# Attention over a graph on one core: 16 instead of 14 of 52 pairs weighted on GpSimd, and another order on TensorE

## The chip, the core and the metric

The kernel runs on one core of a Trainium2 chip. A core has five engines that work beside each other, each through its own queue in order: TensorE (matrix products, its weight loads listed apart), VectorE, ScalarE, GpSimd, and SyncE, which here only starts transfers. Matrix products land in PSUM, everything else lives in SBUF. The metric is the device time of one execution in microseconds (us), the median of three runs.

## The reference

The input is 3327 nodes with 128 features and a dense 0/1 adjacency matrix. Layer 0 is a graph convolution with batch norm and takes little of the time. Layer 1 is an attention whose score gets the adjacency added twice, because it is passed both as spatial and as edge encoding:

```python
x = x + _L0_gnn_ref(h, adj, ...)               # graph convolution, batch norm, relu
h = jnp.maximum(_layernorm(x, axis=-1), 0.0)
q = (h @ Wq.T).reshape(d, n, heads)            # d = 128, n = 3327, heads = 8
k = (h @ Wk.T).reshape(d, n, heads)
v = (h @ Wv.T).reshape(d, n, heads)
a = jnp.einsum('dnh,dmh->dnm', q, k) * d ** (-0.5)
a = softmax(a + adj + adj, axis=2)
out = jnp.einsum('dnm,dmh->dnh', a, v).reshape(n, heads * d)
x = x + out @ Wo.T
```

So there are 128 independent attentions ("d"), each with 3327 queries, 3327 keys and a head size of only 8.

## The kernel before

The first 291 us hold layer 0, the second norm and the first projections. Then `attention()` runs one long unrolled list of steps. It takes the 128 attentions in 32 groups of 4 (`G`), the queries in 7 blocks (six of 512 columns and one of 255), and the keys in 26 chunks of 128. A *pair* is one chunk for two of the four attentions, so a block has 52 pairs; `half` 0 is attentions 0 and 1, `half` 1 is attentions 2 and 3. A block is cut into 13 steps (`SU`) of four pairs: 32 x 7 x 13 = 2912 steps in all. A loop entry is (i, y, s): group, block, step.

One pair goes like this. `product` (L718) makes two score matmuls for a chunk, one for each attention; each uses 32 rows of the array (`rs`, L724: rows 64 half + 32 x), where q and k hold high and low parts of 8 features. They go to one of three score slots in PSUM (`psc`, tile `s`). Then there are two ways to exp(2 x (score + adj)):

- *plain*: VectorE adds the adjacency and a bound to the scores (`add`, L815, tile `d`, L818 in the profile). One ScalarE `Exp` over all plain pairs of a step follows a step later (`late`, L854, L856 in the profile).
- *rest* (`weighted`, L825): ScalarE takes `Exp` of the scores alone (tile `f`, L828), and GpSimd multiplies it by exp(2 adj) (L831), which was stored in DRAM as `wd` and is fetched as `wt`.

`pairs(s)` (L682) says which pairs of a step are which: three plain and one rest, in the last step two and two. Chunks 0 to 18 are plain, chunks from `WC` = 19 on are of the second kind: 14 of 52 pairs. Chunk numbers are arranged so that successive pairs change the half.

The sum over keys is `weigh` (L603): a matmul of a pair's weights with v, one call for each of its two attentions, whose nine output rows lie at 32b, b = 0 to 3, of the block's PSUM bank `av`. In the trace each call is two matmuls. It runs three steps (`LAG`) after the scores: `second(part)` (L776) handles pairs 0 and 1 of the waiting step, then pairs 2 and 3. After a block's last step `finish` (L609) runs in stages through `step()`: VectorE copies `av` to `avs`, TensorE makes four transposes (L619), VectorE divides (L626 to L629), a transfer stores the result.

The order is written out by hand: engines execute in the order in which the loop issues. Within a step (L838 to L852) TensorE gets: scores of the rest pair, scores of plain 0, `second(0)` (four calls), scores of plain 1, scores of plain 2 (or of a second rest pair), guests from `beside`, `second(1)` (four calls). `step()` stands after `second(0)`.

`beside` (L756) lets in guests at fixed steps: projections of the next group (L196, with VectorE's copies and GpSimd's casts behind them) and the output product of the last group (L257, L265). `fetch(x + PRE)` issues transfers two steps ahead on SyncE's queue: `at` (two adjacency chunks) and `wt` (one weight chunk). `weigh_early` and `more_weights` make `wd`: the first `EARLY` = 3 blocks before the loop, the others during group 0. `loads` brings in q, k and v of the next group, with GpSimd casts for k (L180).

Of the kernel before, what the change touches and what calls it, by code (L numbers as in the profile page):

```python
# [22 lines left out]
NC = 26  # L23
T = N * D
NP = NC * P
NB = 512
# [2 lines left out]
HALF = 0.5 / math.sqrt(D)  # L29
SAFE = 30.0  # L30
SU = NC // 2
WC = 19
CH = 4 * NP // D
NG = D // G
EARLY = 3

# [6 lines left out]
def tile_two_layer_gnn(  # L45
# [22 lines left out]
    blocks = [(n0, min(NB, N - n0)) for n0 in range(0, N, NB)]  # L68
# [58 lines left out]
    sets = [tile_set(x) for x in range(2)]  # L127
# [158 lines left out]
    with tc.tile_pool(name="l0", bufs=1) as l0, tc.tile_pool(  # L286
# [125 lines left out]
        for c in range(NC):  # L412
            a = ap.tile([P, 7 * NB], F32, name="a")
# [15 lines left out]
            i = c - 2 * NQ - 5  # L429
            if 0 <= i < NQ - 2 and 4 * i + 4 <= c:  # L430
                spread(i)
        weights = []
        for y, (n0, w) in enumerate(blocks[:EARLY]):
            a = ap.tile([P, 7 * NB], F32, name="a")
            a7 = a.rearrange("p (c n) -> p c n", c=7)
            nc.sync.dma_start(a7[:, :, :w], adjr[:, WC:, n0 : n0 + w])
            weights.append((a7, n0, w))

# [50 lines left out]
        for i, (n0, w) in enumerate(blocks):  # L489
            s = slice(n0, n0 + w)  # L490
# [78 lines left out]
        q, k, v = sets[0]  # L569
# [11 lines left out]
        for x, c in enumerate(range(0, NC, 4)):  # L581
            n = min(4, NC - c)
# [20 lines left out]
    def weigh(tiles, av, w, e, b, c, first, last):  # L603
        nc.tensor.matmul(  # L604
            av[32 * b : 32 * b + H + 1, :w], tiles[2][:, b, c, :], e,
            start=first, stop=last,
        )
# [44 lines left out]
    def attention():  # L652


        with tc.tile_pool(name="adj", bufs=4) as ap, tc.tile_pool(
# [17 lines left out]
            if True:  # L673
                steps = [
                    (i, y, s)
                    for i in range(NG) for y in range(len(blocks)) for s in range(SU)
                ]
# [4 lines left out]
                def pairs(s):  # L682


                    last = s == SU - 1
                    plain = [(j // 2, j % 2) for j in range(3 * s, 3 * s + 3 - last)]
                    rest = [(WC + s // 2, 1 - s % 2)]
                    return plain, rest + ([(NC - 1, 0)] if last else [])


                wanted, have = [], {}
                for x, (i, y, s) in enumerate(steps):
                    n0, w = blocks[y]
                    for c, _ in pairs(s)[0]:
                        if (0, i, y, c // 2) not in have:
                            have[0, i, y, c // 2] = None
                            wanted.append((x, 0, i, y, c // 2))
                    c = pairs(s)[1][0][0]
                    if (1, i, y, c) not in have:
                        have[1, i, y, c] = None  # L700
                        wanted.append((x, 1, i, y, c))

                def fetch(x):
                    while wanted and wanted[0][0] <= x:
# [13 lines left out]
                def product(i, y, c, half):  # L718
                    q, k, _ = sets[i % 2]
                    n0, w = blocks[y]  # L720
                    we = w + w % 2
                    p = psc.tile([P, 2, NB], F32, name="s")
                    for x in range(2):
                        rs = slice(64 * half + 32 * x, 64 * half + 32 * x + 32)  # L724
                        nc.tensor.matmul(  # L725
                            p[:, x, :we], k[rs, c, :], q[rs, n0 : n0 + we],
                            start=True, stop=True,
                        )
                    return p
# [26 lines left out]
                def beside(i, y, s):  # L756


                    for j in [1, 2] if i == 0 else [i + 2] if i + 2 < NG else []:
                        if (y, s) != (0 if i else 3 * (j - 1), 3):  # L760
                            continue
                        hj = wk.tile([P, CH], F32, name="hj")
                        nc.sync.dma_start(hj, hd[:, j * CH : (j + 1) * CH])
                        extra.extend(projections(wk, hj, j, False, ov, low_half[:CH, 1:2]))
                    if s in (8, 11) and extra:
                        drive(extra[0])
                    if s in (9, 12) and extra:
                        drive(extra.pop(0))
                    if s in (7, 10) and extra:
                        drive(extra[0], avs2[(i * len(blocks) + y + 1) % 2])  # L770
                    if (y, s) == (2, 12) and i:
                        extra.extend(outputs(wk, i - 1))

                extra = []

                def second(part):  # L776

                    (i, y, s), es = waiting[0]
                    n0, w = blocks[y]
                    av = avs2[(i * len(blocks) + y) % 2]  # L780
                    ps = sum(pairs(s), [])
                    for j in (0, 1) if part == 0 else (2, 3):
                        c, half = ps[j]
                        for x in range(2):
                            weigh(
                                sets[i % 2], av, w, es[j][:, x, :w], 2 * half + x, c,
                                s == 0 and part == 0, s == SU - 1 and part == 1,
                            )
                    if part:
                        waiting.pop(0)  # L790
                        if s == SU - 1:
                            ending.append(finish(rp, av, at(i), n0, w))

                def step():
                    for g in ending[:1]:
                        if next(g, g) is g:
                            ending.pop(0)

                for x, (i, y, s) in enumerate(steps):
                    n0, w = blocks[y]  # L800
                    fetch(x + PRE)
                    k = x - i * SU * len(blocks) - FROM[i]
                    if k == 0 and i + 1 < NG:
                        pending = loads(sets[(i + 1) % 2], at(i + 1))
                        total = len(pending)

                    while pending and (total - len(pending)) * (SU * len(blocks) - FROM[i] - 4) <= k * total:
                        pending.pop(0)()
                    more_weights(i, y, s)
                    due = len(waiting) == LAG  # L810
                    plain, rest = pairs(s)
                    d = ep.tile([P, 3, 2, NB], F32, name="d")
                    es = [d[:, j] for j in range(len(plain))]

                    def add(j, p):  # L815
                        c = plain[j][0]

                        nc.vector.scalar_tensor_tensor(  # L818
                            d[:, j, :, :w],
                            have[0, i, y, c // 2][:, c % 2, :w]  # L820
                            .unsqueeze(1).to_broadcast([P, 2, w]),
                            SAFE / 2, p[:, :, :w], ALU.min, ALU.add,
                        )

                    def weighted(c, half):  # L825
                        f = fp.tile([P, 2, NB], F32, name="f")
                        p = product(i, y, c, half)
                        nc.scalar.activation(  # L828
                            f[:, :, :w], p[:, :, :w], AF.Exp, scale=2.0
                        )  # L830
                        nc.gpsimd.tensor_tensor(  # L831
                            f[:, :, :w], f[:, :, :w],
                            have[1, i, y, c][:, :w].unsqueeze(1).to_broadcast([P, 2, w]),
                            ALU.mult,
                        )
                        es.append(f)

                    weighted(*rest[0])  # L838
                    if late is not None:
                        late()  # L840
                    add(0, product(i, y, *plain[0]))
                    if due:
                        second(0)
                    step()
                    add(1, product(i, y, *plain[1]))
                    if len(rest) > 1:
                        weighted(*rest[1])
                    else:
                        add(2, product(i, y, *plain[2]))
                    beside(i, y, s)  # L850
                    if due:
                        second(1)  # L852

                    def late(d=d, w=w, n=len(plain)):  # L854
                        flat = d[:, :n].rearrange("p j x n -> p (j x) n")[:, :, :w]
                        nc.scalar.activation(flat, flat, AF.Exp, scale=2.0)  # L856

                    waiting.append(((i, y, s), es))
                late()
                while waiting:  # L860
                    second(0)
                    step()
                    second(1)
                while ending:
                    step()
                for p, b in zip(outputs(wk, NG - 1), (0, 1, 0)):
# [197 lines left out]
```

## Time and profile before

| what | us |
|---|---|
| median of three runs | 10516.94 (10514.26 to 10520.51) |
| the profiled execution's own time | 10527.91 |
| its span, first to last instruction | 10526.1 |
| `d` adds on VectorE, L818, 512 wide, x7296 | 8417.5 busy, 1213 ns each |
| `d` exponentials on ScalarE, L856, three pairs, 512 wide, x2304 | 6398.3 busy, 2777 ns each |
| the same, two pairs, x192 | 372.5 busy, 1940 ns each |
| `f` exponentials on ScalarE, L828, 512 wide, x2688 | 2753.2 busy, 1032 ns each |
| `f` products on GpSimd, L831, 512 wide, x2688 | 6412.7 busy, 2394 ns each |
| score matmuls on TensorE, L725, 512 wide, x19968 | 499 ns each |
| av matmuls from `d`, L604, 512 wide, x29184 | 600 ns each |
| mean granted TensorE clock | 0.986 |

The profile cuts the span in 40 slices; each digit is a busy share in tenths (9 is 90% or more):

```profile
PE   7889999999999999999999999999999999999999
DVE  5789999999999999999999999999999999999998
ACT  4889999999999999999999999999999999999998
POOL 0667777777777777777777777777777777777776
```

PE is TensorE, DVE VectorE, ACT ScalarE, POOL GpSimd; PEld stands for TensorE's weight loads, which are listed as a row of their own. The picture is the same from the second slice to the last, so one block stands for all. Busy times on one engine may overlap slightly: the next instruction begins before the one ahead of it is recorded as ended, and so the distance between starts tells more than a mean duration. In a line of a timeline there are, from the left, the start, the duration of what is merged in the line, the engine, the line of the kernel, the operation, the tile written and the tiles read, the shapes, the count, and in brackets how long the engine was idle before and what ended that.

### The profile page before, as it was taken

To read this page: it belongs to the slowest core of one execution; us is meant where nothing else is said; L and a number is where in the kernel's file an instruction comes from. 1 tells how busy PE (TensorE), PEld (TensorE's weight loads), DVE (VectorE), ACT (ScalarE), POOL (GpSimd) and SP (SyncE) were. 2 spreads that over 40 slices of the span, in tenths; PEclk is the share of its full clock that TensorE was granted. 3 is DMA by queue.
4 is the path that set the end of the run, shared out by engine and by line. 5 is a ranking of instruction groups with operands and counts; after the bars stand their busy time and mean duration, and the time that the engine had idled before them with its cause. 6 is when DMAs were issued, how large, how long until landed. Compare 5 with 4: busy or idle time off the path is not lost. (4 is left out here: it accounts for less than half of the span.)

```text
span 10526.1 us, 186778 instructions
## 1 busy us (share of the span) xinstructions
PE 9922.7 (94%) x72399; PEld 2813.8 (27%) x72399; DVE 9714.9 (92%) x9949; ACT 9948.5 (95%) x6200; POOL 7497.1 (71%) x3868
## 2 busy tenths in 40 slices
PE   7889999999999999999999999999999999999999
PEld 3222222222222222222222222222222222222222
DVE  5789999999999999999999999999999999999998
ACT  4889999999999999999999999999999999999998
POOL 0667777777777777777777777777777777777776
PEclk8899999999999999999999999999999999999999
DMA  7655555555555555555555555555555555555554
GB/s 241 192 168 163 157 168 165 163 162 160 162 166 165 164 162 157 161 170 163 160 162 157 165 170 165 160 158 163 164 169 163 162 163 158 165 165 167 156 152 128
DMA packets 1115761, 1731.67 MB, mean 165 GB/s; under 512 B 198350, under 2 KB 441932, under 8 KB 1107180
## 3 DMA queue, kind: packets, MB, share of 16 engines
q1 hardware_dynamic: 1110478, 1713.99, 56.3%
q8 instruction: 568, 9.31, 0.4%
q10 hardware_dynamic: 4350, 5.64, 0.2%
q14 instruction: 333, 2.73, 0.1%
q0 software_dynamic: 32, 0.00, 0.0%
HBM read 1618.76 MB, written 100.53 MB: 163 GB/s over the span
## 5 line engine op out<-in xcount | busy, mean ns | idle before, releaser
L818 DVE SCALAR_TENSOR_TENSOR d<-at,s 128x1024 f32<-128x1024 f32 x8512 | 9204.3, 1138 | 642.7 <-PE s L725 406.2
L831 POOL TENSOR_TENSOR f<-f,wt 128x1024 f32<-128x1024 f32 (+1 forms) x3136 | 6983.8, 2235 | 2619.1 <-ACT f L828 2572.0
L856 ACT ACTIVATE d<-d 128x3072 f32<-128x3072 f32 (+1 forms) x2912 | 7372.9, 2532 | 73.4 <-DVE d L818 70.5
L604 PE MATMUL av<-d,v 128*9 128x512 f32 x34048 | 5528.5, 569 | 0.1
L725 PE MATMUL s<-q,k 32*128 32x512 f32 x23296 | 4280.7, 482 | 505.7 <-DVE d L818 218.0
L725 PEld LDWEIGHTS s<-q,k 32*128 32x128 f32 x23296 | 1773.9, 182 | 5829.2 <-DVE d L818 3312.2
L828 ACT ACTIVATE f<-s 128x1024 f32<-128x1024 f32 (+1 forms) x3136 | 3014.8, 970 | 313.8 <-PE s L725 252.3
L604 PE MATMUL av<-f,v 128*9 128x512 f32 x12544 | 2864.0, 571 | 0.0
L604 PEld LDWEIGHTS av<-d,v 128*9 128x9 f32 x34048 | 630.7, 88 | 1381.6 <-issue 1265.4
L604 PEld LDWEIGHTS av<-f,v 128*9 128x9 f32 x12544 | 310.6, 88 | 52.9 <-issue 41.0
L180 POOL CAST k<-ks 128x256 fp32r<-128x256 f32 x434 | 284.2, 655 | 0.0
L416 PE MATMUL acc<-a,A 128*128 128x512 f32 (+1 forms) x364 | 151.3, 568 | 24.0 <-ACT A L350 23.3
L619 PEld LDWEIGHTS av<-ident,avs 128*128 128x128 f32 (+1 forms) x864 | 121.1, 208 | 179.9 <-issue 178.8
L226 POOL TENSOR_TENSOR o<-pf,o 104x512 fp32r<-104x512 f32 x124 | 160.4, 1293 | 9.9
L619 PE MATMUL av<-ident,avs 128*128 128x128 f32 (+1 forms) x864 | 163.8, 311 | 0.6 <-DVE avs L612 0.6
L225 POOL CAST o<-pf 104x512 fp32r<-104x512 f32 x124 | 75.8, 611 | 115.3 <-DVE pf L224 59.8
L612 DVE COPY avs<-av 128x512 f32<-128x512 f32 (+1 forms) x224 | 144.2, 644 | 2.8 <-PE av L604 2.8
L423 DVE TENSOR_REDUCE amax<-a 128x1 f32<-128x3327 f32 x26 | 93.7, 3610 | 37.7 <-DMA a<-in_adj 37.7
L416 PEld LDWEIGHTS acc<-a,A 128*128 128x128 f32 x364 | 68.8, 192 | 108.8 <-issue 84.4
L420 ACT ACTIVATE junk<-a 128x3327 bf16<-128x3327 f32 x26 | 77.4, 2977 | 6.6 <-DMA a<-in_adj 6.5
L389 POOL TENSOR_TENSOR sq<-wk 128x512 f32<-128x512 f32 x2 | 2.1, 1040 | 102.3 <-PE aside L390 102.3
L629 DVE TENSOR_TENSOR oq<-av,ri 128x128 f32<-128x128 f32 (+1 forms) x224 | 64.1, 286 | 7.7
(120 smaller groups left out, 952.0 us busy)
## 6 DMA issues: line engine op xcount, KB each, us to landing
at<-in_adjT SPq DMA_DIRECT2D x1728, 512.0 KB
wt<-wd SPq DMA_DIRECT2D x1344, 256.0 KB
at<-in_adjT SPq DMA_DIRECT2D x288, 255.0 KB
ks<-kT SPq DMA_DIRECT2D x496, 104.0 KB
q<-qT SPq DMA_DIRECT2D x496, 104.0 KB
at<-in_adjT SPq DMA_DIRECT2D x192, 256.0 KB
a<-in_adj SPq DMA_DIRECT2D x26, 1663.5 KB
wt<-wd SPq DMA_DIRECT2D x224, 127.5 KB
```

The source lines that it names most:

```text
L180: nc.gpsimd.tensor_copy(k[:, c : c + n, half * 64 : half * 64 + 64], ks.bitcast(F32).rearrange("g (p c) -> g c p", c=NC)[:, c : c + n, :],)
L226: nc.gpsimd.tensor_tensor(o[:CH, 1], f[:CH], o[:CH, 0].bitcast(F32), ALU.subtract)
L416: nc.tensor.matmul(acc[i][:, :w], A[:, c, :], a[:, n0 : n0 + w], start=(c == 0), stop=(c == NC - 1),)
L423: nc.vector.tensor_reduce(amax[:, c : c + 1], a[:, :N], AX.X, ALU.max, apply_absolute_value=True)
L604: nc.tensor.matmul(av[32 * b : 32 * b + H + 1, :w], tiles[2][:, b, c, :], e, start=first, stop=last,)
L612: nc.vector.tensor_copy(avs[:, :w], av[:, :w])
L619: nc.tensor.transpose(pt[:R, j, :], avs[:, j : j + (R - 1) * J + 1 : J], ident)
L725: nc.tensor.matmul(p[:, x, :we], k[rs, c, :], q[rs, n0 : n0 + we], start=True, stop=True,)
L818: nc.vector.scalar_tensor_tensor(d[:, j, :, :w], have[0, i, y, c // 2][:, c % 2, :w] .unsqueeze(1).to_broadcast([P, 2, w]), SAFE / 2, p[:, ...
L828: nc.scalar.activation(f[:, :, :w], p[:, :, :w], AF.Exp, scale=2.0)
L831: nc.gpsimd.tensor_tensor(f[:, :, :w], f[:, :, :w], have[1, i, y, c][:, :w].unsqueeze(1).to_broadcast([P, 2, w]), ALU.mult,)
L856: nc.scalar.activation(flat, flat, AF.Exp, scale=2.0)
```

## The change

`pairs(s)` now reads a table `kinds`. Steps 4, 8 and 12 (`DOUBLE`) have two plain and two rest pairs, the other ten three and one; so 36 pairs are plain and 16 rest, and `WC` becomes 18. `beside` moves VectorE's part of the guests into steps 8 and 12 (their later part to step 9 and to step 0 of the next block), and the matmul of the second guest from step 10 to 11.

On TensorE the order in a step becomes: `second(0)` (two calls), scores of plain 0, `second(1)`, `step()`, `second(2)`, scores of plain 1, `second(3)`, scores of plain 2 (or of the second rest pair), scores of the next step's first rest pair (`coming`), guests. `second` now handles one pair a call.

The early weights cover two blocks instead of three, 1024 columns in three pieces of 342 with 8 chunks each, in place of three pieces of 512 with 7 chunks; block 2 is left to the loop.

```diff
-WC = 19
+WC = 18
-EARLY = 3
+DOUBLE = (4, 8, 12)
+EARLY = 2
...
-        for y, (n0, w) in enumerate(blocks[:EARLY]):
+        w = -(-EARLY * NB // 3)
+        for n0 in range(0, EARLY * NB, w):
             a = ap.tile([P, 7 * NB], F32, name="a")
-            a7 = a.rearrange("p (c n) -> p c n", c=7)
+            a7 = a.rearrange("p (c n) -> p c n", c=8)
...
                 def pairs(s):
-                    last = s == SU - 1
-                    plain = [(j // 2, j % 2) for j in range(3 * s, 3 * s + 3 - last)]
-                    rest = [(WC + s // 2, 1 - s % 2)]
-                    return plain, rest + ([(NC - 1, 0)] if last else [])
+                    return kinds[s]
+
+                kinds = []
+                for s in range(SU):
+                    j, k = (sum(len(x[i]) for x in kinds) for i in range(2))
+                    n = 2 if s in DOUBLE else 1
+                    kinds.append((
+                        [(x // 2, x % 2) for x in range(j, j + 4 - n)],
+                        [(WC + x // 2, 1 - x % 2) for x in range(k, k + n)],
+                    ))
...
-                    c = pairs(s)[1][0][0]
-                    if (1, i, y, c) not in have:
-                        have[1, i, y, c] = None
-                        wanted.append((x, 1, i, y, c))
+                    for c, _ in pairs(s)[1]:
+                        if (1, i, y, c) not in have:
+                            have[1, i, y, c] = None
+                            wanted.append((x, 1, i, y, c))
...
-                    if s in (8, 11) and extra:
+                    if s in (8, 12) and extra:
                         drive(extra[0])
-                    if s in (9, 12) and extra:
+                    if s == 9 and extra or s == 0 and (y or i) and begun:
                         drive(extra.pop(0))
-                    if s in (7, 10) and extra:
+                        begun.pop()
+                    if s in (7, 11) and extra:
+                        begun.append(1)
                         drive(extra[0], avs2[(i * len(blocks) + y + 1) % 2])
...
-                def second(part):
+                def second(j):
+                    if not due:
+                        return
                     (i, y, s), es = waiting[0]
...
-                    for j in (0, 1) if part == 0 else (2, 3):
-                        c, half = ps[j]
-                        for x in range(2):
-                            weigh(
-                                sets[i % 2], av, w, es[j][:, x, :w], 2 * half + x, c,
-                                s == 0 and part == 0, s == SU - 1 and part == 1,
-                            )
-                    if part:
+                    c, half = ps[j]
+                    for x in range(2):
+                        weigh(
+                            sets[i % 2], av, w, es[j][:, x, :w], 2 * half + x, c,
+                            s == 0 and j < 2, s == SU - 1 and j >= 2,
+                        )
+                    if j == 3:
                         waiting.pop(0)
...
+                def first(x):
+                    i, y, s = steps[x]
+                    return product(i, y, *pairs(s)[1][0])
+
+                coming = first(0)
                 for x, (i, y, s) in enumerate(steps):
...
-                    def weighted(c, half):
+                    def weighted(c, p):
                         f = fp.tile([P, 2, NB], F32, name="f")
-                        p = product(i, y, c, half)
...
-                    weighted(*rest[0])
+                    weighted(rest[0][0], coming)
                     if late is not None:
                         late()
+                    second(0)
                     add(0, product(i, y, *plain[0]))
-                    if due:
-                        second(0)
+                    second(1)
                     step()
+                    second(2)
                     add(1, product(i, y, *plain[1]))
+                    second(3)
                     if len(rest) > 1:
-                        weighted(*rest[1])
+                        weighted(rest[1][0], product(i, y, *rest[1]))
                     else:
                         add(2, product(i, y, *plain[2]))
+                    if x + 1 < len(steps):
+                        coming = first(x + 1)
                     beside(i, y, s)
-                    if due:
-                        second(1)
```

More of the change, by code (lines that the diff above doesn't have):

```diff
@@ L772, in beside @@
                         extra.extend(outputs(wk, i - 1))
-                extra = []
-                def second(part):
+                extra, begun = [], []
+                def second(j):
+                    if not due:
+                        return
                     (i, y, s), es = waiting[0]
@@ L859, in attention @@
                 late()
+                due = True
                 while waiting:
-                    second(0)
+                    for j in range(4):
+                        second(j)
                     step()
-                    second(1)
                 while ending:
```

## The prediction

> **What bounds the kernel now.** I read the page's busy times and groups first, then the list of waits, then the timelines of ScalarE, of TensorE's weight loads and of its matmuls in single steps of the loop (a step is four pairs; a block has 13 steps, a group 7 blocks, there are 32 groups).
>
> ```profile
> PE 9922.7 (94%) x72399; PEld 2813.8 (27%) x72399; DVE 9714.9 (92%) x9949; ACT 9948.5 (95%) x6200; POOL 7497.1 (71%) x3868
> PEld s L725 <- DVE d L818: 3312.2, 4433, 6.4
> PEld s L725 <- ACT f L828: 1197.0, 1922, 11.8
> ```
>
> Three engines look full. But TensorE's loads for the scores `s` stand still 3312.2 us for VectorE and 1197.0 us for ScalarE, which free the score slots: those two set the pace, and TensorE's 94% is not work. ScalarE's timeline in full-width steps:
>
> ```profile
> 3101.64 1.08 ACT L828 ACTIVATE f<-s 128x1024 f32<-128x1024 f32 x1
> 3102.54 2.84 ACT L856 ACTIVATE d<-d 128x3072 f32<-128x3072 f32 x1
> 3105.20 1.08 ACT L828 ACTIVATE f<-s 128x1024 f32<-128x1024 f32 x1
> ```
>
> Start to start, `f` takes 0.90 and `d` 2.66 us: 3.56 a step. VectorE has three adds of about 1.16 (three in 3.48 us at 3100.09), 3.5 us, and stretches the steps that bring it a copy or a reciprocal. Successive `avs` copies, one a block, lie 46.96 and 48.33 us apart (3048.64, 3095.60, 3143.93), against 12 x 3.56 + 3.65 = 46.4 us of ScalarE.
>
> What TensorE needs by itself, from its weight loads, the first instruction of each phase:
>
> ```profile
> 3101.79 0.12 PEld L604 LDWEIGHTS av<-d,v 128*9 128x9 f32 x8 [0.24 <-issue]
> 3102.77 0.19 PEld L725 LDWEIGHTS s<-q,k 32*128 32x128 f32 x4 [0.86 <-DVE d L818]
> 3103.20 0.10 PEld L604 LDWEIGHTS av<-d,v 128*9 128x9 f32 x3 [0.25 <-issue]
> ...
> 3104.18 0.18 PEld L725 LDWEIGHTS s<-q,k 32*128 32x128 f32 x2 [0.86 <-DVE ri L627]
> 3105.45 0.18 PEld L725 LDWEIGHTS s<-q,k 32*128 32x128 f32 x2 [1.08 <-DVE d L818]
> 3105.88 0.12 PEld L604 LDWEIGHTS av<-d,v 128*9 128x9 f32 x8 [0.24 <-issue]
> 3106.85 0.19 PEld L725 LDWEIGHTS s<-q,k 32*128 32x128 f32 x4 [0.86 <-ACT f L828]
> ```
>
> An `av` phase (two pairs, four `weigh` calls, eight matmuls, since each call is two) takes 3101.79 to 3102.77 = 0.98 us. A score phase of four matmuls takes 0.43 (3102.77 to 3103.20). A score phase of which only two were left takes 0.43 as well (3105.45 to 3105.88). So the number of matmuls in a phase is not its price. The matmuls say why:
>
> ```profile
> 3103.21 0.60 PE L604 MATMUL av<-d,v 128*9 128x512 f32 x2
> 3103.22 0.60 PE L604 MATMUL av<-f,v 128*9 128x512 f32 x2
> 3103.64 0.60 PE L604 MATMUL av<-d,v 128*9 128x512 f32 x2
> 3103.65 0.60 PE L604 MATMUL av<-f,v 128*9 128x512 f32 x2
> ```
>
> Four start together, and 0.43 later the other four: the four calls lie in four column strips (32b, b = 0 to 3) and run side by side; only the two matmuls of one call follow each other. That a call alone is no cheaper is seen at a projection:
>
> ```profile
> 3013.99 0.26 PEld L196 LDWEIGHTS av<-wv,hj 128*104 128x104 f32 x2 [0.24 <-issue]
> 3015.02 0.10 PEld L604 LDWEIGHTS av<-d,v 128*9 128x9 f32 x3 [0.78 <-issue]
> ```
>
> One call, 1.03 us. In 255-wide blocks (at 10489.92, 10490.24 and 10490.79 in the same timeline) the phases are 0.32 and 0.55. From widths 512 and 256 a score phase is about 0.21 fixed plus 0.22 of streaming.
>
> Before, a step is two cycles of (score, av): 2 x 1.41 = 2.82 us, and a block 26 x 1.41 + 0.67 (four transposes, 3002.09 to 3002.76) + 1.3 of guests = 38.6 us against 47 to 48. TensorE has 9 us to spare in each block.
>
> **What the Trainium skill says.** "TensorE: Matmul & The Clock Gate", Part 3, The mechanism: matmuls on different row or column strips run concurrently, but all start and end in program order. The trace agrees with the first (starts 0.01 apart). By the second, four calls share the time only if nothing stands between them. "TensorEngine Tiling (Array Packing)", Key Properties: changing the tiling mode drains the array. The trace agrees: `s` (32*128) never overlaps `av` (128*9), and each change shows a bare load, 0.19 or 0.12. "Trainium Kernel Development and Optimization", Performance Expectations: matmul busy time is a bad measure of distance to the limit; here 94% busy holds 38.6 us of need in 48.
>
> **The change, part by part.**
>
> *Order on TensorE.* Before: av of two pairs twice a step. After: av j0 | s plain0 | av j1, j2 | s plain1 | av j3 | s last and s coming | ... So three cycles of phases a step, not two. j0 and j3 stand alone, two calls in two strips, each call's two matmuls still serial: 2 x 0.43 + 0.12 = 0.98, as a full phase. s plain0 and plain1 alone: 0.43 each, as measured. No run of before has a lone av pair: below it could be 0.43 if half-filled phases went at double speed, above 0.98; I take 0.98, for the projection above goes no faster alone. Full width: 39 cycles x 1.41 = 55.0 us a block. 255 wide: 39 x 0.87 = 33.9.
>
> *Halves.* From `kinds`: in 10 of 13 steps (all but 4, 8, 12) the last pair of a step and `coming` have the same half, so the same two row strips, and run one after the other. Unseen in before, where every score phase has both halves. Below 0 (if they overlap after all), above 0.40 (0.19 load and 0.22 streaming: the page's same section lets a load overlap only other row strips); I take 0.21, streaming alone, since in the first layer's row of matmuls loads of the same strips are hidden (one start each 0.43, load 0.19). 10 x 0.21 = 2.1 us; 255 wide 1.1. In the double steps j1 and j2 have the same half, so the same column strips: 0.86 more, at s = 7, 11 and 2, three steps later: 2.6 us; 255 wide 1.3. Bounds 0.8 to 1.0.
>
> *Transposes.* `step()` now stands between second(1) and second(2), so at s = 4 the four transposes part j1 from j2: 0.98 more (0.55 narrow), beside their own 0.67.
>
> Sum: 55.0 + 2.1 + 2.6 + 0.98 + 0.67 = 61.3 us full, 33.9 + 1.1 + 1.3 + 0.55 + 0.67 = 37.5 narrow. A group 6 x 61.3 + 37.5 = 405.3, 32 of them 12,970. Guests as before: 186 projections x 1.04 = 193, 31 outputs x (2 x 0.50 + 1.93) = 91 (3063.84 to 3064.34, 3110.78 to 3112.71). Outside the loop: 297 us before its steps run and 20 after the last av (the chain ends 10505.98 to 10526). 12,970 + 284 + 317 = 13,571 span, 1.8 more as the profiled run's time, and the median of the runs lies 11 below that: 13,560.
>
> *VectorE.* 36 adds, not 38: 2 x 1.16 = 2.3 us a block less, and copies moved into the steps with two adds (8 and 12). Worth nothing: 36 x 1.16 + 1.4 (`finish`) + 0.8 of guests = 44 us, beside 61 of TensorE.
>
> *ScalarE.* 10 x 3.56 + 3 x (0.90 + 1.83 + 0.91) = 46.5 us, hidden. *GpSimd.* 16 x 2.39 = 38.3 us and its casts, hidden.
>
> *Slots.* With three score slots each product waits for the third before it. By the phases above (step of 4.42): plain0 at 0.98, plain1 at 2.39, last at 3.80. Add 0 ends at about 2.7, add 1 at 4.1, add 2 at 5.5; plain0 of the next step comes at 5.4 and needs add 1: free. plain1 at 6.8 needs add 2: free. The next `coming`, behind which that step's j0 is queued, needs add 0: long done. In a step with a 0.68 copy add 2 ends near 5.7: still free. I count no stall; if this cover failed by 0.1 a step it would be 290 us.
>
> *Loads and start.* `at` fetches 9, not 10, a block, `wt` 8, not 7: the same columns in all, on the same SP queue in the same places. DMA is at half use. The early weights go as three DMAs of 8 x 342 for 7 x 512, and in group 0 block 2's are made in the loop, some 8 ScalarE calls of 1.15: at most 9 us, hidden by a lag of three steps. Early part: within 10 us either way; I take 0.
>
> **Rivals.**
> 1. *Partial overlap* (12,580): lone av pairs or same-half scores cost less than a phase. With 0 for the halves of the scores (6 x 2.1 x 32 + 1.1 x 32 = 440 less) and 0.10 less in each lone av phase (2 x 13 x 0.10 x 6 x 32, half of it narrow: 540 less). Against it: both prices come from starts in the trace.
> 2. *Faster*: TensorE stays hidden, and what VectorE gives up counts. It needs lone phases that cost what their matmuls weigh, half: 26 x (0.49 + 0.21) = 18.2 us less, 43.1 a block, under ScalarE's 46.5. A block then goes from 48.4 on average ((319.0 a group - 28.5 narrow) / 6) to 46.5: 1.9 x 192 = 365 us, so 10,150. It decides at 46.5 us of TensorE per block; with only the av half as dear it is 48.6, which is no change. For it: VectorE's stretched steps are real. Against: the 1.03 of a lone call and the 0.43 of a lone score pair.
> 3. *A further wait comes on top* (14,050 to 14,500): 0.40 for same-half scores (+400), or a stall of 0.1 to 0.2 a step. For it: only half a score phase lies between some frees and their use if ScalarE slips.
>
> **How the numbers follow.** Forecast 0.79, rival 1 0.09, rival 2 0.04, rival 3 0.08. The forecast's own width: scores' halves 0 to 0.40 gives -440 to +400, so 13,120 to 13,960; the start 10. Reaching toward the rivals, 12,900 to 14,050. A change under 0.2% can't be told here. Slower 0.95 (forecast, 1, 3), faster 0.04, within 0.2% 0.01 between them.
>
> **What would show it.** Three score starts and three av starts a step instead of two; av loads of a lone pair to the next score load near 0.97; a step near 4.4 and near 5.3 at s = 2, 7 and 11; VectorE's and ScalarE's busy shares near 73% and their idle before `d` and `f` put down to `s`; idle before score loads put down to VectorE mostly gone, beside the 0.86 in which av streams. If lone av phases last 0.5 us, or score loads still wait for VectorE longer than av streams, I am wrong.

## The result and the profile after

The changed kernel takes 13532.4 us (median of 4 runs, 13526.66 to 13554.16) against 10517.81 for the kernel before (4 runs): 1.287 times as long, 95% interval 1.2848 to 1.2893. The forecast was 13,560. The profiled run has a span of 13532.9. Its mean granted TensorE clock is 0.996, against 0.986 before, so a lower clock is not the cause.

The page of the changed kernel, part 1 (busy time and share of the span) and part 4 (the chain that ended last, by engine and by line):

```profile
PE 13394.6 (99%) x72399; PEld 3320.8 (25%) x72399; DVE 9698.5 (72%) x9501; ACT 10411.6 (77%) x6652; POOL 8433.9 (62%) x4316
...
PE 97%; DVE 2%; DMA 1%; ACT 1%; issue 0%; POOL 0%; ACTq 0%; DVEq 0%; POOLq 0%; SPq 0%
PE av L606 63%; PE s L733 30%; PE av L197 1%; DVE d L835 1%; PE av L621 1%; PE acc L417 1%; PE av L266 0%; ACT f L844 0%; PE av L258 0%; DMA q<-qT 0%; DMA xs<-in_x 0%; ACT A L351 0%; ACT junk L421 0%; PE aside L407 0%; DMA a<-in_adj 0%
```

The number of matmuls is the same as before, 72399. VectorE fell from 92% of the span to 72%, ScalarE from 95% to 77%. The chain of waits, which in the kernel before could be followed back only through the last 42 us, now runs through TensorE from end to end: `av` 63%, scores 30%.

From the lists of waits, first of the kernel before, then of the changed kernel (engine and tile that waited, what ended the wait, us in total, times, longest):

```profile
DVE d L818 <- PE s L725: 406.2, 785, 2.3
ACT f L828 <- PE s L725: 252.3, 380, 7.6
```

```profile
DVE d L835 <- PE s L733: 3258.0, 5084, 3.3
ACT f L844 <- PE s L733: 2743.1, 2617, 8.1
...
PEld s L733 <- DVE d L835: 1044.3, 1258, 6.9
```

The direction of waiting has turned. Before, VectorE waited 406.2 us for scores and ScalarE 252.3; now VectorE waits 3258.0 us and ScalarE 2743.1 us for TensorE. The idle time before score loads, 3312.2 us put down to VectorE before and 1044.3 now, is in neither kernel all a stall: a score load is idle for 0.86 us while `av` streams in any case, and the list names whichever release came last. What TensorE really loses is seen from the first load of a phase to the first load of the next, over the whole trace. In full blocks of the kernel before a score phase lasts 0.78 us on average (4985 phases), where 0.43 is enough: TensorE waited for its slots. In the changed kernel a lone score pair lasts 0.43 on average (4986) and a lone `av` pair 0.96 (5374), with hardly any spread: in full blocks TensorE waits for next to nothing.

The timeline of TensorE's weight loads in the changed kernel, one step and parts of the next (start, duration, tile, count of loads, idle before):

```profile
3107.57 0.30 PEld L733 LDWEIGHTS s<-q,k 32*128 32x128 f32 x4 [0.86 <-issue]
3108.23 0.10 PEld L606 LDWEIGHTS av<-d,v 128*9 128x9 f32 x4 [0.37 <-issue]
3109.20 0.18 PEld L733 LDWEIGHTS s<-q,k 32*128 32x128 f32 x2 [0.86 <-issue]
3109.63 0.12 PEld L606 LDWEIGHTS av<-d,v 128*9 128x9 f32 x8 [0.25 <-issue]
3110.60 0.18 PEld L733 LDWEIGHTS s<-q,k 32*128 32x128 f32 x2 [0.86 <-issue]
3111.03 0.11 PEld L606 LDWEIGHTS av<-f,v 128*9 128x9 f32 x4 [0.24 <-issue]
3111.99 0.30 PEld L733 LDWEIGHTS s<-q,k 32*128 32x128 f32 x4 [0.86 <-issue]
...
3114.05 0.10 PEld L606 LDWEIGHTS av<-d,v 128*9 128x9 f32 x4 [0.24 <-issue]
3114.48 0.10 PEld L606 LDWEIGHTS av<-f,v 128*9 128x9 f32 x2 [0.33 <-issue]
...
3115.87 0.18 PEld L733 LDWEIGHTS s<-q,k 32*128 32x128 f32 x2 [0.86 <-DVE d L835]
```

Read start to start. A phase of one av pair (x4 loads, 3108.23 to 3109.20 and 3111.03 to 3111.99) lasts 0.97 and 0.96 us; the phase of two pairs between them (x8, 3109.63 to 3110.60) 0.97. Half the work, the same price. A lone score pair takes 0.43 (3109.20 to 3109.63). The two score pairs of equal half take 0.66 (3107.57 to 3108.23) instead of 0.43. The step from 3107.57 to 3111.99 is 4.42 us. The last three lines show the av phase of two middle pairs that share their column strips; the waiting step that is worked off here is one of the double steps, those with two rest pairs (4, 8 and 12). The second pair's loads (from `f`) come only 0.43 after the first pair's, and the phase lasts 1.82 (3114.05 to 3115.87).

Four transposes that part the two middle pairs, same view:

```profile
3124.69 0.56 PEld L621 LDWEIGHTS av<-ident,avs 128*128 128x128 f32 x4 [0.86 <-issue]
3125.37 0.11 PEld L606 LDWEIGHTS av<-d,v 128*9 128x9 f32 x4
3126.34 0.18 PEld L733 LDWEIGHTS s<-q,k 32*128 32x128 f32 x2 [0.86 <-issue]
```

0.68 us of transposes, and behind them 0.97 for the pair they cut off.

Successive `avs` copies of full blocks with two projections lie 63.06 and 63.03 us apart (3282.23, 3345.29, 3408.32); at the same places of a group the kernel before has 48.34 and 48.35.

### The profile page after: what moved, and what is told of

The parts are those of the page before. It is cut to its first block, busy times and chain, and to the rows that moved or that the text cites. A ratio compares the mean times of both kernels' runs of the same rounds, so it can differ in the third digit from the quotient of the medians.

```text
span 13532.9 us, 187751 instructions
## 1 busy us (share of the span) xinstructions
PE 13394.6 (99%) x72399; PEld 3320.8 (25%) x72399; DVE 9698.5 (72%) x9501; ACT 10411.6 (77%) x6652; POOL 8433.9 (62%) x4316
## 4 chain that ended last, share of the span: by engine, by line
PE 97%; DVE 2%; DMA 1%; ACT 1%; issue 0%; POOL 0%; ACTq 0%; DVEq 0%; POOLq 0%; SPq 0%
PE av L606 63%; PE s L733 30%; PE av L197 1%; DVE d L835 1%; PE av L621 1%; PE acc L417 1%; PE av L266 0%; ACT f L844 0%; PE av L258 0%; DMA q<-qT 0%; DMA xs<-in_x 0%; ACT A L351 0%; ACT junk L421 0%; PE aside L407 0%; DMA a<-in_adj 0%
## 5 line engine op out<-in xcount | busy, mean ns | idle before, releaser
L835 DVE SCALAR_TENSOR_TENSOR d<-at,s 128x1024 f32<-128x1024 f32 x8064 | 9167.4, 1144 | 3667.4 <-PE s L733 3258.0
L847 POOL TENSOR_TENSOR f<-f,wt 128x1024 f32<-128x1024 f32 (+1 forms) x3584 | 7932.2, 2228 | 4806.8 <-ACT f L844 4796.9
L874 ACT ACTIVATE d<-d 128x3072 f32<-128x3072 f32 (+1 forms) x2912 | 6986.0, 2399 | 86.8 <-DVE d L835 61.0
L606 PE MATMUL av<-d,v 128*9 128x512 f32 x32256 | 5903.7, 564 | 0.0
L844 ACT ACTIVATE f<-s 128x1024 f32<-128x1024 f32 (+1 forms) x3584 | 3379.7, 962 | 2856.6 <-PE s L733 2743.1
L733 PE MATMUL s<-q,k 32*128 32x512 f32 x23296 | 4720.2, 459 | 42.0 <-ACT f L844 24.9
L733 PEld LDWEIGHTS s<-q,k 32*128 32x128 f32 x23296 | 1871.6, 182 | 7019.4 <-issue 4611.6
L606 PE MATMUL av<-f,v 128*9 128x512 f32 x14336 | 3478.9, 564 | 0.0
L606 PEld LDWEIGHTS av<-f,v 128*9 128x9 f32 x14336 | 438.8, 89 | 1068.4 <-issue 910.3
L197 PE MATMUL av<-wq,hj 128*104 128x512 f32 x124 | 68.5, 635 | 0.0
```

What stands on the lines that cost most here:

```text
L197: nc.tensor.matmul(bank[:CH], hj, wqk[s][:, e * NB : (e + 1) * NB], start=True, stop=True)
L606: nc.tensor.matmul(av[32 * b : 32 * b + H + 1, :w], tiles[2][:, b, c, :], e, start=first, stop=last,)
L733: nc.tensor.matmul(p[:, x, :we], k[rs, c, :], q[rs, n0 : n0 + we], start=True, stop=True,)
L835: nc.vector.scalar_tensor_tensor(d[:, j, :, :w], have[0, i, y, c // 2][:, c % 2, :w] .unsqueeze(1).to_broadcast([P, 2, w]), SAFE / 2, p[:, ...
L844: nc.scalar.activation(f[:, :, :w], p[:, :, :w], AF.Exp, scale=2.0)
L847: nc.gpsimd.tensor_tensor(f[:, :, :w], f[:, :, :w], have[1, i, y, c][:, :w].unsqueeze(1).to_broadcast([P, 2, w]), ALU.mult,)
```

## The experiments

My theory before the runs: the loss is the order on TensorE, priced by phases and strips, and nothing else. Rivals: the double steps or the 16 pairs cost it; the look-ahead product and its slot cost it; TensorE waits for ScalarE or VectorE. Where no interval is given, a kernel ran once; the four runs of the changed kernel lie within 27 us.

**The partition with the order of before** (e1_old_order). The changed kernel, with this edit:

```diff
-                    weighted(rest[0][0], coming)
+                    weighted(rest[0][0], product(i, y, *rest[0]))
...
-                    second(0)
                     add(0, product(i, y, *plain[0]))
+                    second(0)
                     second(1)
                     step()
-                    second(2)
                     add(1, product(i, y, *plain[1]))
-                    second(3)
...
-                    if x + 1 < len(steps):
-                        coming = first(x + 1)
                     beside(i, y, s)
+                    second(2)
+                    second(3)
```

> The changed kernel's 16 weighted pairs, double steps and guests, with TensorE's order of before (two av phases of four calls, no score product ahead). Theory: the loss is all in the order. TensorE needs 26 x 1.41 + 2 = 38.7 us a block again and hides; ScalarE's 46.5 us a block sets the pace and VectorE has 2.3 us a block less: 10,150 if every stall goes, about 10,350 if half of them do. Rival, the partition itself costs: 10,600 or more. Rival, the loss is in the partition and not in the order: over 13,000.

Measured: 10465.98 us, ratio to before 0.9951 (0.9938 to 0.9965). The whole loss is gone with the order, and the partition with its guests' places is a small gain. It is smaller than I expected; see below.

**Guests where they were** (e6_old_order_old_guests). As e1, with `beside` of the kernel before:

```diff
-                    if s in (8, 12) and extra:
+                    if s in (8, 11) and extra:
                         drive(extra[0])
-                    if s == 9 and extra or s == 0 and (y or i) and begun:
+                    if s in (9, 12) and extra:
                         drive(extra.pop(0))
-                        begun.pop()
-                    if s in (7, 11) and extra:
-                        begun.append(1)
+                    if s in (7, 10) and extra:
```

> As e1_old_order, but the guests (projections and outputs) at their places of before, steps 7 to 12. Tells what placing VectorE's copies into the steps with two adds is worth: a copy of 0.68 us in a step with three adds makes VectorE's step 4.2 us against ScalarE's 3.56. Theory: 0.6 us for each of 9 guest parts a group, x 32 = about 170 us slower than e1_old_order. Rival, the lag of three steps hides the copies anyway: no difference.

Measured: 10510.02 us, ratio 0.9997 (0.9989 to 1.0005): 44 us slower than e1. The 16 weighted pairs without the guests' new places bring nothing that can be measured; the 0.5% is the guests' place beside them. The size lay between my two expectations, 170 us and none; why it is 44 these runs don't show.

**Phases paired, product still ahead** (e5_paired_ahead). The changed kernel, with this edit:

```diff
                     second(0)
+                    second(1)
                     add(0, product(i, y, *plain[0]))
-                    second(1)
                     step()
                     second(2)
+                    second(3)
                     add(1, product(i, y, *plain[1]))
-                    second(3)
```

> The changed kernel, with second(0) and second(1) together before the scores of plain 0, and second(2) and second(3) together before those of plain 1; the score of the next step stays ahead. Two av phases and two score phases a step: 2 x 0.98 + 0.43 + 0.65 = 3.04 us, under ScalarE's 3.56. Theory (phases are what costs): 10,300 to 10,700. Rival, the product ahead with its slot is what slows: near 13,000.

Measured: 10493.0 us, ratio 0.9984 (0.9976 to 0.9993). With the product still one step ahead, but the av calls in two groups of four, the 3000 us are gone. The look-ahead is not the cost. Nor is the work of the other engines: VectorE, ScalarE, GpSimd and the transfers do here just what they do in the changed kernel, and are done in 10493 us.

**The order alone** (e2_new_order_only). The kernel before in everything but TensorE's order; as an edit of the changed kernel:

```diff
-WC = 18
+WC = 19
-DOUBLE = (4, 8, 12)
+DOUBLE = (12,)
-EARLY = 2
+EARLY = 3
...
+        (early weights and beside() as in the kernel before)
```

> The kernel before (14 weighted pairs, its guests, its early weights) with the changed kernel's order on TensorE alone. Theory: three phase cycles a step cost the same here: 39 x 1.41 = 55.0, same-half scores in 12 steps 2.5, same-half av pairs in one step 0.9, transposes 0.98 + 0.67: 60.0 us a block, 36.9 narrow, in all about 13,270. Rival, the double steps are what costs: close to 10,520.

Measured: 13267.59 us. The order alone, without more weighted pairs, costs 26%. The remaining 265 us up to the changed kernel are the two more double steps' shared column strips less two same-half score groups a block: added up over the two traces, av phases last 354 us longer in the changed kernel and score phases 95 us less. (The sums, 60.0 and 61.3 us a block, give 269.)

**Other halves** (e3_halves). The changed kernel with the halves of weighted pairs swapped:

```diff
-                        [(WC + x // 2, 1 - x % 2) for x in range(k, k + n)],
+                        [(WC + x // 2, x % 2) for x in range(k, k + n)],
```

> The changed kernel with the halves of all weighted pairs swapped (x % 2 for 1 - x % 2), so that the last product of a step and the one ahead lie in different row strips in every step, and the two middle av pairs in different column strips in every step. Theory: same strips run one after the other, 2.1 + 2.6 us a block and 2.4 in narrow ones: 980 us less, 12,550. Rival, only the av part is real: 12,990. Rival, strips don't matter once phases are apart: 13,530.

Measured: 12545.18 us. One small change of arithmetic, the same count of instructions on each engine in part 1 of the page, 987 us. From the loads' timeline of this kernel, a step of it:

```profile
3117.05 0.19 PEld L733 LDWEIGHTS s<-q,k 32*128 32x128 f32 x4 [0.86 <-issue]
3117.49 0.10 PEld L606 LDWEIGHTS av<-d,v 128*9 128x9 f32 x4 [0.24 <-issue]
...
3121.25 0.19 PEld L733 LDWEIGHTS s<-q,k 32*128 32x128 f32 x4 [0.86 <-issue]
```

The four-score phase is 0.44 (3117.05 to 3117.49), where it was 0.66, and the step 4.20 (3117.05 to 3121.25), where it was 4.42. Both parts of the strips' price are in the 987, and the two traces tell them apart: added up from each phase's first load to the next phase's, score phases last 450 us less than in the changed kernel (440 in the sum) and av phases 534 less (540 in the sum).

**Transposes elsewhere** (e4_transposes). The changed kernel with

```diff
-                    second(1)
                     step()
+                    second(1)
                     second(2)
```

> The changed kernel with step() ahead of second(1), so that the transposes no longer part the two middle av pairs. Theory: one av phase of 0.98 us a block less (0.55 narrow): 206 us, 13,326. Rival, the transposes' own change of tiling is what costs there: no difference.

Measured: 13328.37 us, 204 less than the changed kernel. The transposes' price was the pair that they cut off: the trace has 223 av phases fewer, one for nearly each of the 224 blocks, and av phases last 202 us less in all.

**Less work on ScalarE, in both orders** (e8_after_less_scalar, e9_old_order_less_scalar). The changed kernel and e1, each with the exponential of only the first plain pair of a step, the others left out:

```diff
-                        flat = d[:, :n].rearrange("p j x n -> p (j x) n")[:, :, :w]
+                        flat = d[:, :1].rearrange("p j x n -> p (j x) n")[:, :, :w]
```

> The changed kernel with the exponential taken of the first plain pair of a step only, the others left out: ScalarE 1.7 us a step less. Theory (TensorE alone sets the pace): 13,530, as before the cut. Rival (TensorE waits for ScalarE's slots or for d): below 13,000.

> e1_old_order with the same exponentials left out. Theory (with the order of before ScalarE sets the pace, then VectorE at 44 us a block and 24 narrow): 32 x (6 x 44 + 26) + 320 = 9,600 to 9,900. Rival (something else than ScalarE holds e1_old_order at its time): 10,300 or more.

Measured: 13539.27 us and 10040.26 us. The pages, part 1, first of e8, then of e9:

```profile
PE 13395.4 (99%) x72399; PEld 3319.2 (25%) x72399; DVE 9696.5 (72%) x9501; ACT 6097.2 (45%) x6652; POOL 8400.8 (62%) x4316
```

```profile
PE 9585.2 (95%) x72399; PEld 2698.9 (27%) x72399; DVE 9270.3 (92%) x9501; ACT 6143.7 (61%) x6652; POOL 8404.9 (84%) x4316
```

In the changed kernel 4300 us of ScalarE's work can go and the time stays (7 us more, one run, within the 27 us of the changed kernel's own runs): ScalarE is not in the way. With the order of before the same cut brings 426 us, so there it is. It brings less than I expected (9,600 to 9,900): VectorE, at 92%, is the next candidate, but no run here tests it, and what holds the last 140 us I didn't separate.

**Guests split** (e7_guests_split). In e1 a stall of ScalarE was left. From its timelines, TensorE first, then ScalarE:

```profile
3208.56 1.10 PE L197 MATMUL av<-wk,hj 128*104 128x512 f32 x2
3209.59 1.05 PE L606 MATMUL av<-f,v 128*9 128x512 f32 x8
3210.57 0.51 PE L733 MATMUL s<-q,k 32*128 32x512 f32 x4
```

```profile
3211.17 1.02 ACT L843 ACTIVATE f<-s 128x1024 f32<-128x1024 f32 x1 [0.44 <-PE s L733]
```

A projection takes TensorE from 3208.56 to 3209.59, the av phase behind it and then the scores are late, and ScalarE stands idle for 0.44 us before `f`. The edit of e1 cuts each guest in two, one half in steps 6 or 10 and one in 7 or 11 (the output product likewise, with one `drive` more where guests are driven at once; the cut shows the projection):

```diff
-        nc.tensor.matmul(
-            bank[:CH], hj, wqk[s][:, e * NB : (e + 1) * NB], start=True, stop=True
-        )
-        yield
+        for b in (0, NB // 2):
+            nc.tensor.matmul(
+                bank[:CH, b : b + NB // 2], hj,
+                wqk[s][:, e * NB + b : e * NB + b + NB // 2], start=True, stop=True
+            )
+            yield
...
-                    if s in (7, 11) and extra:
+                    if s in (7, 11) and begun:
+                        drive(extra[0])
+                    if s in (6, 10) and extra:
                         begun.append(1)
```

> As e1_old_order, with each guest's TensorE work cut in two and spread over two steps (a projection as two matmuls of 256 columns at steps 6 and 7 or 10 and 11, outputs likewise). In e1_old_order ScalarE stands 0.44 us before f in the step after a guest's 1.03 us on TensorE, because 2.82 + 1.03 is more than its 3.56. Theory: half a guest, about 0.6 us, fits in the 0.74 to spare: 0.44 x 9 guests a group x 32 = 127 us less than e1_old_order, 10,340. Rival: the stall comes from elsewhere (casts, narrow blocks), no change, 10,466.

Measured: 10398.94 us, ratio 0.9887 (0.9870 to 0.9903): faster than both kernels, and 67 us under e1 where I expected 127. In the list of waits of this kernel

```profile
ACT f L850 <- PE s L738: 176.3, 426, 8.0
```

ScalarE's wait for scores is 176.3 us, where the list of e1 has 285.4: part of that stall was TensorE's guests, and about half of what I had counted for it was there to be had. What the remaining 176.3 comes from is not separated.

## Why the prediction was right

By its own steps:

- *TensorE has room before, but not for a third cycle of phases.* Right, though one reading behind it was too strong. The 3312.2 and 1197.0 us before score loads are not all standstill: the prediction's own line at 3102.77 is put down to VectorE, and its 0.86 us is `av` streaming. The room is in the score phases, 26 x (0.78 - 0.43) = 9 us a block, as said. e8 shows that ScalarE doesn't set the pace of the changed kernel, e5 that the other engines' work fits into 10493 us, and the chain is 97% TensorE; e9 against e1 shows that with the order of before TensorE's own work was not what set the pace: it stayed as it was, and the time fell.
- *A lone av pair costs a full phase.* This was the step with the widest doubt, 0.43 to 0.98. The Trainium skill's page "TensorE: Matmul & The Clock Gate" (Part 3, The mechanism) says that matmuls start and end in program order, and the trace agrees: a pair that is parted from its neighbour runs by itself, as the one of 0.97 us at 3108.23 above. The price came from the projection's 1.03 us. Measured 0.96 to 0.97. One reading beside it was too neat: `s` and `av` do overlap a little in the records (an `av` matmul from 3103.65 lasts 0.60, to 3104.25, and the score load starts at 3104.18); the sums go by starts and are not touched by it.
- *The total.* The predicted span was 38 us too long, and that it is so little is in part luck. From its `avs` copies a group takes 411.9 us on average, where the sum with its guests gives about 414: some 70 us too long in 32 groups, nearly all of it lone av phases (26 x 0.015 = 0.4 us a block). About 30 us were missing elsewhere; where is not separated.
- *A lone score pair costs 0.43.* Measured 0.43.
- *Same-half scores 0.21 more, same-half av pairs 0.86 more.* Measured 0.23 (0.66 - 0.43) and 0.85 (1.82 - 0.97), and e3 removes both at once for 987 us against 980 in the sum.
- *The transposes part a phase.* 206 in the sum, 204 in e4.
- *VectorE, ScalarE, GpSimd and the loads hidden.* VectorE at 72% as said; ScalarE at 77%, said near 73%. No slot stall shows: score loads follow their av phase at once in the steps above, and the means over the whole trace leave no room for one.
- *The rivals.* Partial overlap (12,580) and the further wait (14,050 and more) didn't come. The faster one asked for half-price lone phases, and the profile shows full-price ones.

What it had wrong is a side estimate: that a block without VectorE's stalls would fall from 48.4 to 46.5 us. e1 has removed the other cause of loss and gains 0.5%, not 365 us. The waits explain it: in the kernel before ScalarE waited 70.5 us in all for VectorE before `d`, and 252.3 us for scores before `f`; in e1 it is 11.3 and 285.4. VectorE's relief took away the smaller wait. Most of what lay between 48.4 and 46.5 was ScalarE's wait for scores, not for VectorE. Splitting TensorE's guests took 109 us of that wait away (e7); the cause of the rest stays open.

## What to carry to other kernels

Count TensorE's work in phases, not in matmuls: calls in different strips share one phase only while they stand next to each other in the program, so a finer interleave can cost a whole phase for each cut. Before reordering, write down for each group of neighbours which row or column strips it fills; a swap of halves was worth 7% here with the same instruction counts. A TensorE that was 94% busy had a fifth of its time to spare here, and one that was 99% busy had none: the distance between the first loads of successive phases, set against the same phase where nothing holds it up, told them apart better than the busy share.

## What the runs showed that I had not expected

Two things were worth less than I expected: VectorE's relief (e6 and e1) and the end of the guests' stall (e7, about half). And e9 came out at 10040 us, between the 9,600 to 9,900 of one expectation and the 10,300 of the other.

The bound of 0.40 us for same-half scores came from a sentence of the Trainium skill's page "TensorE: Matmul & The Clock Gate", Part 3, The mechanism: loads overlap running matmuls only where the row strips differ. (A little above, the same section also lets a load go ahead into a background weight buffer.) Here the second pair's loads start 0.11 us after the first pair's, at 3107.68 against 3107.57, in the same two row strips and while the first pair's matmuls run, and the 0.23 us more is about what the prediction's widths give for streaming alone, 0.22. So that sentence by itself does not hold in this case; whether the background buffer is the reason no run here shows.
